# Two weight splits put off in a graph attention kernel, output sums moved behind a maximum, one split moved to GpSimd

## The chip, the cores and the metric

The kernel runs on one core of a Trainium2 chip. The metric is device time in microseconds (us) of one execution; lower is better. The profile is one execution recorded by the hardware profiler. Five engines work side by side, each through its own instructions in order: TensorE (PE; its weight loads are shown as PEld), VectorE (DVE), ScalarE (ACT), GpSimd (POOL) and SyncE (SP), which here only issues DMA transfers.

## The reference

A pre-norm graph attention layer on 384 nodes of 1024 features, with 16 heads of 64. Cut to what matters:

```python
h = maximum(layernorm(x), 0)
q = h @ wq.T + bq;  k = h @ wk.T + bk;  v = h @ wv.T + bv
q2 = (q @ wiq.T + biq).reshape(N, H, D).transpose(1, 0, 2)      # k2, v2 likewise
mask = full((N, N), -inf); mask[src, dst] = softplus(edge_type_weights)[edge_type - 1]
# diagonal cells without an edge get the fourth weight
attn = softmax(q2 @ k2.T / sqrt(D) + mask)
out = (attn @ v2) as (N, 1024)
return x + out @ wo.T + bo
```

## The kernel before

**Precision.** Every operand of the large products is cut into a high and a low part in a fast 32-bit matmul type, and each product is made of three matmuls (high by high, high by low, low by high; `mm3`, lines 367 to 369). A weight matrix comes in eight chunks of 128x1024 (512 KB). `load(w)` (line 65) starts the transfer of chunk `w` on SyncE's queue into one of three `raw` buffers; `split_hi(w)` (line 77) makes the high part on ScalarE, `split_lo(w)` (line 82) the low part on VectorE or, if so told, on GpSimd. Split chunks lie in four `whl` buffers. Because `raw` has three buffers, `load(w + 4)` fills the buffer of chunk `w + 1` and must wait for that chunk's low part.

**Chunks.** Numbers 0 to 31 are those of v, q, the second v and k. From `W0` = 32 the q2 and k2 chunks alternate: 32 + 2p is q2 of head pair p, 33 + 2p is k2. Numbers 48 to 55 are the output weights wo.

**Score phase.** A loop runs over steps i. Step i issues the scores S(i) (two matmuls, line 694) of head i // 3 and node block i % 3 in one of two PSUM banks `s`, then the masked maximum of step i-1 (`do_ttr`, line 700, VectorE), the exponential of i-2 (line 704, ScalarE), the normalization of i-3 (line 709, GpSimd), the transpose of i-5 (line 714), the split of the transposed probabilities of i-6 (lines 723 and 724) and, every third step, the product with v2 (line 731) and its evacuation (lines 741 and 742). Ahead of and behind S(i), a generator fills TensorE's time with other products, by a credit of about 8 per step: first `fill_qk` (the q2 and k2 chunks, 3 credits a block of `mm3`), then `fill_o` (the output product, 4 credits a block). Before step 0 `fill(PRE)` issues 28 blocks: chunks 32 to 34 and half of chunk 35.

**Work around a chunk.** At the start of chunk w's blocks `qk_head(w)` is put on a list, and run at once before step 0 or at the end of the step (`run_tasks`). It issues `load(w + 4)`, splits chunk w + 2 (low part on GpSimd for odd numbers, `PAR` = 1, on VectorE for even ones) and finishes the chunk before it: `qk_done` evacuates that chunk's sum to `nat` (lines 377 and 378), then rearranges it by four DMAs into `qs` (lines 557 to 560) or `ks` (line 567), which the scores read. All DMAs of the phase but four stand in SyncE's one queue in the order written.

**Output product.** It is made in two passes over the wo chunks: 0 to 3, then 4 to 7, for six output halves (three node blocks by two halves of 512 columns). The first pass ends for half a with `ysum(a)` (line 654, VectorE), which adds the PSUM sum onto a copy of x + bo in SBUF and so frees one of the three banks `g`. The last blocks of the first pass may start from step 43 (`XSTEP` + 3); x + bo is read back at step 40. `wo_prep(k)` splits wo chunk k at the steps in `WSTEPS`, k = 2 to 7 at 37, 40, 42, 44, 47, 51: the low part goes to GpSimd for k in `OPOOL` = (2, 3, 6), the high part to VectorE for k = 2. It then loads chunk k + 2.

## Time and profile before

| | us |
|---|---|
| median of three runs | 303.34 |
| lowest, highest of them | 301.37, 303.49 |
| the profiled execution | 302.19 |
| its span in the profile | 300.5 |

A line of the profile's timeline gives start and duration in us from the start of the span, engine, source line, operation, output<-inputs and shape, and in brackets the idle time before it and what ended it. A few matmul records can be missing, so a single gap of one matmul means nothing. The score phase lies between 160.85 (S0) and 270.9 (S47). What the engines did there, in two stretches around the changed places (columns: busy us and count for each engine, granted clock of TensorE, share of the DMA engines, GB/s):

```profile
165.00:170.00 5.00, 5.00 (x29) 4.70 (x29) 3.40 (x13) 3.33 (x8) 3.12 (x3) 1.00 1.06 223
260.00:265.00 5.00, 4.77 (x25) 3.62 (x23) 4.83 (x10) 3.25 (x9) 0.83 (x1) 1.00 0.69 260
```

The columns are PE, PEld, DVE, ACT, POOL. In the first the DMA engines are full, in the second VectorE nearly so and GpSimd nearly idle.

### The profile page before, as it was taken

The page shows a single profiled execution, that of the slowest core. Times are in us where ns is not written, and L with a number is a line of the kernel's source. Part 1 is how long each engine was busy: PE and PEld are TensorE (multiplying, and loading weights), DVE is VectorE, ACT ScalarE, POOL GpSimd, SP SyncE. Part 2 cuts the span into 40 slices and gives each one's busy share as a digit, 9 for nine tenths or more (in the row PEclk, how much of TensorE's full clock was granted, in tenths as well). Part 3 has the DMA queues.
Part 4 walks back from the last instruction along what each step waited for, and adds up shares of the span by engine and source line. Part 5 has one row for each costly group of instructions (what it writes and reads, how often), then busy time and mean ns, then how long its engine had stood idle before and what let it go on. Part 6 is the DMA issues. An engine that isn't in the chain of part 4 may idle for free.

```text
span 300.5 us, 4961 instructions
## 1 busy us (share of the span) xinstructions
PE 293.1 (98%) x1649; PEld 276.1 (92%) x1649; DVE 200.5 (67%) x492; ACT 154.9 (52%) x289; POOL 155.7 (52%) x164
## 2 busy tenths in 40 slices
PE   7899999999999999999999999999999999999995
PEld 5699999999988889999999999999999998888884
DVE  2959986655956463788865576767576757696523
ACT  3874644333422213554325667777777767676310
POOL 5865766271555785730033737373746467566210
PEclk9999999999999999999999999999999999999999
DMA  7899754642686668475369997646565636910005
GB/s 233 284 297 381 281 164 171 228 143 70 217 238 224 193 217 242 142 274 198 115 169 244 217 221 173 166 127 180 155 170 139 174 81 174 381 41 0 2 0 209
DMA packets 22377, 55.12 MB, mean 183 GB/s; under 512 B 4816, under 2 KB 8400, under 8 KB 22352
## 3 DMA queue, kind: packets, MB, share of 16 engines
q1 hardware_dynamic: 19968, 52.42, 57.7%
q0 software_dynamic: 2064, 1.80, 2.0%
q10 hardware_dynamic: 320, 0.59, 0.8%
q8 instruction: 13, 0.21, 0.3%
q14 instruction: 12, 0.10, 0.1%
HBM read 40.39 MB, written 4.97 MB: 151 GB/s over the span
## 4 chain that ended last, share of the span: by engine, by line
PE 95%; DMA 2%; DVE 1%; ACT 0%; issue 0%; SPq 0%
PE g L369 21%; PE g L367 21%; PE g L368 21%; PE s L694 6%; PE a L731 6%; PE t L714 5%; PE s L369 2%; PE s L368 2%; PE s L367 2%; DMA g<-in_x_dram 2%; PE t L369 2%; PE t L367 2%; PE t L368 2%; PE g L414 1%; PE a L369 1%; PE a L367 1%
## 5 line engine op out<-in xcount | busy, mean ns | idle before, releaser
L367 PE MATMUL g<-g,whl 128*128 128x384 f32 x312 | 106.4, 341 | 0.0
L369 PE MATMUL g<-g,whl 128*128 128x384 f32 x312 | 104.5, 335 | 0.0
L368 PE MATMUL g<-g,whl 128*128 128x384 f32 x312 | 104.2, 334 | 0.0
L228 POOL DMA_INDIRECT tab<-val,idx x51 | 57.6, 1129 | 40.3 <-issue 11.3
L77 ACT ACTIVATE whl<-raw 128x1024 fp32r<-128x1024 f32 x51 | 53.4, 1051 | 31.7 <-PE g L369 20.1
L709 POOL TENSOR_TENSOR e<-e,s 128x384 f32<-128x384 f32 x48 | 39.2, 830 | 41.2 <-DVE s L708 32.9
L368 PEld LDWEIGHTS g<-g,whl 128*128 128x128 f32 x312 | 58.7, 188 | 0.0
L367 PEld LDWEIGHTS g<-g,whl 128*128 128x128 f32 x312 | 58.6, 188 | 0.0
L369 PEld LDWEIGHTS g<-g,whl 128*128 128x128 f32 x312 | 58.5, 188 | 0.0
L82 DVE TENSOR_TENSOR whl<-raw,whl 128x1024 fp32r<-128x1024 f32 x41 | 50.2, 1224 | 9.6 <-ACT whl L77 7.9
L82 POOL TENSOR_TENSOR whl<-raw,whl 128x1024 fp32r<-128x1024 f32 x11 | 26.5, 2412 | 35.6 <-ACT whl L77 31.8
L383 ACT ACTIVATE g<-f,bc 128x384 fp32r<-128x384 f32 x24 | 14.8, 618 | 53.1 <-DVE f L382 46.8
L704 ACT ACTIVATE e<-e,s 128x384 f32<-128x384 f32 x48 | 29.4, 612 | 13.0 <-DVE s L700 13.0
L724 DVE TENSOR_TENSOR pt<-t,pt 128x384 fp32r<-128x384 f32 x48 | 26.4, 550 | 13.9 <-ACT pt L723 13.3
L723 ACT ACTIVATE pt<-t 128x384 fp32r<-128x384 f32 x48 | 23.2, 484 | 13.9 <-PE t L714 13.3
L700 DVE CUSTOM_DVE_ANT_0 e<-s,ma 128x384 f32<-128x384 f32 x48 | 26.3, 550 | 2.0 <-PE s L694 1.8
L694 PE MATMUL s<-ks,qs 128*128 128x384 f32 x96 | 25.3, 344 | 0.3 <-DVE s L700 0.2
L714 PE MATMUL t<-ident,e 128*128 128x128 f32 x144 | 23.5, 271 | 0.0
L382 DVE TENSOR_TENSOR f<-g,rrow 128x384 f32<-128x384 f32 x24 | 13.3, 555 | 13.5 <-PE g L369 7.6
L714 PEld LDWEIGHTS t<-ident,e 128*128 128x128 f32 x144 | 18.8, 140 | 3.1
L378 DVE SCALAR_TENSOR_TENSOR nat<-g,bc,nat 128x384 fp32r<-128x384 f32 x16 | 9.9, 618 | 16.4 <-ACT nat L377 14.4
L731 PE MATMUL a<-pt,vhl 128*128 128x384 f32 x96 | 20.8, 351 | 0.0
(147 smaller groups left out, 414.8 us busy)
## 6 DMA issues: line engine op xcount, KB each, us to landing
ks<-nat SPq DMA_DIRECT2D x30, 192.0 KB
raw<-in_wv_dram SPq DMA_DIRECT2D x8, 512.0 KB
raw<-in_wq_dram SPq DMA_DIRECT2D x8, 512.0 KB
raw<-in_wiv_dram SPq DMA_DIRECT2D x8, 512.0 KB
raw<-in_wk_dram SPq DMA_DIRECT2D x8, 512.0 KB
raw<-in_wiq_dram SPq DMA_DIRECT2D x8, 512.0 KB
raw<-in_wik_dram SPq DMA_DIRECT2D x8, 512.0 KB
raw<-in_wo_dram SPq DMA_DIRECT2D x8, 512.0 KB
```

The lines of the kernel that those rows point to most:

```text
L77: nc.scalar.activation(dst[0], raw[w], AF.Copy)
L82: (eng or nc.vector).tensor_tensor(lo, raw[w], hi.bitcast(F32), OP.subtract)
L228: nc.gpsimd.indirect_dma_start(out=tabs[c // RNG], out_offset=bass.IndirectOffsetOnAxis(ap=idx[:, c:c + 1], axis=0), in_=val[:, c:c + 1], ...
L367: nc.tensor.matmul(ps, lhi, rhi, start=first, stop=False)
L368: nc.tensor.matmul(ps, lhi, rlo, start=False, stop=False)
L369: nc.tensor.matmul(ps, llo, rhi, start=False, stop=last)
L694: nc.tensor.matmul(ps[:, :N], qs[:, o, t * 128:(t + 1) * 128], ks[:, o, s, :], start=(s == 0), stop=(s == 1))
L704: nc.scalar.activation(es[i], es[i], AF.Exp, bias=s[:, 0:1], scale=-1.0, accum_out=s[:, 1:2])
L709: nc.gpsimd.tensor_tensor(es[i], es[i], s[:, 2:3].to_broadcast([128, N]), OP.mult)
L714: nc.tensor.transpose(ps[:, k * 128:(k + 1) * 128], es[i][:, k * 128:(k + 1) * 128], ident)
L724: nc.vector.tensor_tensor(lo, pv, hi.bitcast(F32), OP.subtract)
L731: nc.tensor.matmul(ps[:, :N], vhl[:, k, p, 2 * o:2 * o + 2, :], pts[h][:, s, k, :], start=(k == 0 and s == 0), stop=(k == 2 and s == 1))
```

## The change

1. `qk_head` for chunks 35 and 36 no longer splits chunks 37 and 38 at once. It loads, finishes the chunk before, and notes the split for a later step: chunk 37 for the end of step 2 (noted before step 0), chunk 38 for the end of step 3 (noted in step 1).
2. `ysum(a)` of the first pass is noted in a list, and `flush_y` issues it behind the masked maximum of the step, or before a bank is taken for a new output half, whichever comes first.
3. wo chunk 4's low part goes to GpSimd: `OPOOL` = (2, 3, 4, 6).

TensorE's instructions and SyncE's DMAs stand in the same order in both programs.

```diff
+    defer = []
+
+    def qk_split(w):
+        split_hi(w)
+        split_lo(w, nc.gpsimd if w % 2 == PAR else None)
+
     def qk_head(w):
         first = w - W0 < 3
         if not first:
             load(w + 4)
+            if w - W0 < 5:
+                pendq.pop(0)()
+                defer.append((now[0] + 6 - w + W0, w + 2))
+                return
             split_hi(w + 2)
...
-    PAR, OPOOL, ODVE = 1, (2, 3, 6), (2,)
+    PAR, OPOOL, ODVE = 1, (2, 3, 4, 6), (2,)
...
+    ysums = []
+
+    def flush_y():
+        while ysums:
+            ysum(ysums.pop(0))
+
...
             if k == 0:
+                flush_y()
                 oacc[OT[a]] = bank("g")
             omm(*OT[a], k)
             if k == KH - 1:
-                ysum(a)
+                ysums.append(a)
             yield 4
...
             if k == KH:
+                flush_y()
                 oacc[OT[a]] = bank("gggss"[a])
...
             do_ttr(i - 1)
+        flush_y()
         if 0 <= i - 2 < S:
             do_exp(i - 2)
...
         run_tasks()
+        while defer and defer[0][0] <= i:
+            qk_split(defer.pop(0)[1])
```

## The prediction

> **What bounds the kernel now.** Read the page first, then TensorE's and its weight loads' timeline wherever a start is late, then the queues that release those starts.

> ```profile
> span 300.5 us, 4961 instructions
> PE 293.1 (98%) x1649; PEld 276.1 (92%) x1649; DVE 200.5 (67%) x492; ACT 154.9 (52%) x289; POOL 155.7 (52%) x164
> PE 95%; DMA 2%; DVE 1%; ACT 0%; issue 0%; SPq 0%
> ```

> The last line is the chain of waits: 95% of it is TensorE. The most a change of order can win is therefore the sum of TensorE's late starts. In the timeline a 384-column matmul follows the one before it after 0.173 us and a 512-column one after 0.23 us, at granted clock 1.00; a start later than that is a stall. The score steps have few, and these are those near the change:

> ```profile
> 166.19 0.30 PEld L694 LDWEIGHTS s<-ks,qs 128*128 128x128 f32 x2 [0.30 <-DVE s L700]
> 172.05 0.30 PEld L694 LDWEIGHTS s<-ks,qs 128*128 128x128 f32 x2 [0.36 <-issue]
> ...
> 262.30 0.40 PE L369 MATMUL g<-whl,g 128*128 128x512 f32 x1
> 262.92 0.62 PE L694 MATMUL s<-ks,qs 128*128 128x384 f32 x2 [0.23 <-DVE s L700]
> ...
> 264.86 0.40 PE L369 MATMUL g<-whl,g 128*128 128x512 f32 x1
> 265.24 0.62 PE L694 MATMUL s<-ks,qs 128*128 128x384 f32 x2
> ```

> The reader is to see four scores (L694) that start late: S3 (166.19), S6 (172.08 on TensorE), S44 (262.92), S45 (265.24). In start-to-start steps they cost: S3 0.319 - 0.173 and 0.284 - 0.173 for its second matmul, 0.26 together; S6 0.408 - 0.173 = 0.23; S44 0.625 - 0.23 and 0.282 - 0.173, 0.50; S45 0.374 - 0.23 and 0.11, 0.25. Scores have two PSUM banks, so S(i) waits for the masked maximum (L700) of i-2. VectorE shows what that one stands behind:

> ```profile
> 164.45 1.21 DVE L82 TENSOR_TENSOR whl<-raw,whl 128x1024 fp32r<-128x1024 f32 x1
> 165.58 0.55 DVE L700 CUSTOM_DVE_ANT_0 e<-s,ma 128x384 f32<-128x384 f32 x1
> ...
> 259.76 1.23 DVE L82 TENSOR_TENSOR g<-raw,g 128x1024 fp32r<-128x1024 f32 x1 [0.39 <-ACT g L77]
> 260.91 1.49 DVE L654 TENSOR_TENSOR g<-g,g 128x512 f32<-128x512 f32 x2
> 262.31 0.55 DVE L700 CUSTOM_DVE_ANT_0 e<-s,ma 128x384 f32<-128x384 f32 x1
> ```

> S3 waits behind the low part of chunk 38; S44 behind a wo low part and two output sums. S6 is another matter: its maximum was done at 170.7, and the profile says only "issue". It also waits for its K rows. By the trace's semaphore events the two DMAs with the first half of pair 1's K landed at 171.04 and 171.99, and S6 loaded its weights at 172.05: **a DMA wait**. SyncE's queue issued them so:

> ```profile
> 162.88 0.53 SPq L65 DMA_DIRECT2D raw<-in_wiq_dram  x1
> 164.56 2.64 SPq L567 DMA_DIRECT2D ks<-nat  x4
> 167.30 0.66 SPq L65 DMA_DIRECT2D raw<-in_wik_dram  x1
> ```

> [...]the load issued at 162.88 landed at 170.25, and K behind it at 171.04, 171.99, 173.15, 174.20. [...]The trace has a case: beside a GpSimd operation that took 2.00 us (L747, others 1.01), VectorE's L82 took 1.71 (usually 1.22). Maximum and output sum read one input from PSUM.

> **Part 1: splits of chunks 37 and 38 put off.** TensorE's and SyncE's orders stay as they were. On ScalarE hi(37) moves behind exponential 0 and hi(38) behind exponential 1; on VectorE lo(38) moves behind maxima 1 and 2; GpSimd's lo(37) keeps its place but waits for hi(37). Worked forward with durations of before:
> - ScalarE: pair 1's evacuations (L377) no longer stand behind the two splits, of which hi(38) waited for its load until 162.35. K of pair 1 (chunk 35) is evacuated when its matmuls end, about 162.4 instead of 163.3; exponential 0 about 162.9 to 163.6; hi(37) (1.05) to 164.6; exponential 1 to 165.3; hi(38) to 166.3.
> - VectorE: maximum 1 follows K's low evacuation, ending about 164.1 instead of 166.1. S3 starts on time: **-0.26**. lo(38) runs 166.3 to 167.5; behind it maximum 3 ends at 168.0, S5 (169.6 before) wants it at 169.3: covered. Chunk 38 is first multiplied near 174: covered.
> - GpSimd: lo(37) 164.6 to 167.0 (2.40) instead of 159.7 to 162.2. Normalizations 0 and 1 follow, done 168.7 (before 168.4); the first transpose needs one at 170.3: covered. lo(39) starts some 0.2 later. Chunk 37 is first multiplied with its low part at 168: 1 us of cover, the thinnest.
> - SyncE: load(40) takes chunk 37's buffer, so it waits for lo(37): issued about 167.0, not 162.9. Behind it in the queue are the four K DMAs of pair 1 (four times 0.66), load(41) (which also waits for lo(38), 167.5, less than its turn at 170.3), four Q DMAs of pair 2, load(42). K is then issued from 167.6 instead of 164.56. That is **the new cost**. Bounds for the K landing that S6 needs: the early one by a quiet stretch, where K issued at 190.94 had its second landing at 194.66, 3.72 later: 171.3. The late one is the whole shift of load(40), 171.99 + 4.1 = 176.1. Between: before, load(40) was issued into a backlog (DMA busy share about 1.0 from 160 to 180), and the Q DMAs ahead of it landed up to 168.04; a load in a quiet queue takes 3.25 (145.10 to 148.37). So load(40) lands near 170.3, about where it did, and K 0.8 and 1.0 after one another: second half at 172.1, range 171.8 to 172.8. I take 172.1.
> - S6 would be reached at 172.08 - 0.23 - 0.26 = 171.6; with K at 172.1 it starts at about 172.2. The 0.26 is given back in a longer stall: **S6 moves by +0.1** (at best -0.5, likely at most +0.8). Pair 2's Q and K have slack: K was issued at 176.15, when its evacuation was ready, and the queue has caught up by then (about 173.9 for load(42)).

> **Part 2: output sums behind the maximum.** Maximum 42 needs S42 (done 258.55) and VectorE is free at 259.4 with lo(wo 4) gone: it ends at 260.0, not 262.9. S44 starts on time: **-0.50**. First sum: its matmuls end near 260.65, so 260.65 to 261.3. Second: ends near 261.65, so to 262.35 as before. Then reciprocal, low part, head sum, third sum (0.69) to 264.15, and maximum 43 (0.55) at 264.1 to 264.7, 0.5 earlier than before. TensorE wants it for S45 0.50 earlier too: the 0.25 stall of S45 stays. The fourth output half takes the first one's bank, so its first matmul waits for the first sum (261.3); TensorE gets there near 262.9: covered. The later sums stand beside a maximum that was done 0.7 us before its score (269.8 for 270.53) or beside one that frees a bank for no score: nothing.

> **Part 3: lo(wo 4) on GpSimd.** 2.40 us at 259.7 to 262.1, in an idle stretch of 3.50 us (before 263.11, L709). Normalization 40 follows at 262.5. The chunk is used after 267. SyncE's last wo load waits for it, about 1.2 later (issued near 262.2); it is split at 278.76: covered. VectorE's work beside it has one PSUM input[...], and L82 on GpSimd at 255.64 slowed no maximum. A slowing would cost at most 0.5 (1.71 - 1.22)[...].

> **Sum**: +0.1 - 0.50 = -0.4 us (bounds -1.0 to +3.6). On the profiled execution 302.19 (span 300.5 and 1.69 around it) this is 301.8. That execution lies 1.15 below the median of three, 303.34; the median of all four is 302.77. I set the sum against that one: **302.4**.

> **Rivals.**
> - A, as worked out: -0.8 to +0.2 with the range of the landing, around 302.4. Chance 0.6.
> - B, K lands by 171.5: S6 keeps the whole gain, about -1.0, 301.8 on the same base. For it: the quiet 3.72. Against: load(40) goes first. 0.12.
> - C, slower: K stays behind load(40) late, at S6 alone. The change in time is (landing - 171.99) - 0.50, so it decides from a landing of 172.5. With 173.5 it is +1.0, 303.8; with the full shift +3.6, 306.4. For it: four microseconds of later issue. Against: the backlog that load(40) sat in anyway. 0.23, of which 0.03 is over 1%.
> - D, the stall of S44 passes to S45 whole, because the sums still come before maximum 43: +0.1, 302.9. Against: every term in that VectorE chain moves forward. 0.05.

> 1%, 3 us, is about what a measurement can tell here; runs of before differ by 2.1. All of A, B and D and most of C lie within it. A gain over 3 us has no place: the four stalls sum to 1.24. I leave 0.02 for the measurement. Faster 0.02, same 0.95, slower 0.03. The range adds the scatter of the runs to A and part of B and C: **301.0 to 304.2**.

> **What would show it.** S3 after 0.17, S44 after 0.23; S6's stall longer than 0.36 with load(40) issued near 167; S45 still late; GpSimd's low parts (L82) 13 instead of 12. Wrong if S6 starts later than 173 (C), or if chunk 37's multiplication waits for GpSimd.

## The result, and the profile after

| | before | after |
|---|---|---|
| median, us (runs) | 302.56 (22) | 304.81 (22) |
| lowest, highest | 301.37, 303.82 | 303.00, 307.99 |
| the profiled execution, span | 302.19, 300.5 | 303.63, 301.9 |

The change makes the kernel slower: ratio 1.0073, interval [1.0054, 1.0091], 2.25 us by the medians. The ratio is that of the runs without the two slowest, 307.70 and 307.99; the medians are of all runs. The page of the kernel after begins:

```profile
span 301.9 us, 4965 instructions
PE 292.5 (97%) x1649; PEld 276.2 (91%) x1649; DVE 200.4 (66%) x491; ACT 155.2 (51%) x289; POOL 162.0 (54%) x165
PE 92%; DMA 4%; ACT 1%; POOL 1%; DVE 1%; SPq 1%; issue 0%
```

TensorE does the same work in the same time and carries 92% of the chain of waits instead of 95%; DMA has 4% instead of 2%. In the timeline the scores have moved to line 712, the masked maximum to 718, the normalization to 727, the output sum to 664. Around S6 it shows:

```profile
165.36 2.41 POOL L82 TENSOR_TENSOR whl<-raw,whl 128x1024 fp32r<-128x1024 f32 x1 [8.97 <-ACT whl L77]
166.85 1.99 DVE L82 TENSOR_TENSOR whl<-raw,whl 128x1024 fp32r<-128x1024 f32 x1 [0.81 <-ACT whl L77]
167.79 0.33 SPq L65 DMA_DIRECT2D raw<-in_wiq_dram  x1
168.22 3.25 SPq L567 DMA_DIRECT2D ks<-nat  x4
...
172.13 0.34 PE L369 MATMUL g<-g,whl 128*128 128x384 f32 x1
173.94 0.59 PE L712 MATMUL s<-ks,qs 128*128 128x384 f32 x2 [1.47 <-DMA ks<-nat]
```

This execution runs 0.72 us later than that of before from S0 on (161.57 against 160.85), which is no work of the change: the experiment below that only exchanges two transfers of the kernel before at a later place starts as late. In the four profiles at full clock with no edit ahead of S0 (before, and three of the experiments) S0 lies anywhere from 160.85 to 161.70. So 0.72 is subtracted when the two are compared. GpSimd makes chunk 37's low part at 165.36; SyncE can issue load(40) only at 167.79, and the four K DMAs of pair 1 behind it from 168.22. S6 follows the matmul at 172.13 after 1.81 us, where before took 0.408. By the trace's semaphore events load(40) landed at 172.30, the two first K halves at 173.07 and 173.85.

The DMA view for 166 to 175 us has 40 slices of 0.225 us; a digit is the busy share of the 16 DMA engines in tenths. Before:

```profile
DMA  8998999999999999999999999999997997999999
```

After:

```profile
DMA  5321000000008959898799999899999999999999
```

The reader is to see the zeros: from about 166.9 to 168.7 the DMA engines had nothing to do, because SyncE's queue stood still at the wait for chunk 37's low part.

At the other place, the maximum comes first and both sums follow. The score at 262.36 is S43, S44 is the one at 264.43, 0.234 after the matmul before it, and S45 the one at 266.66:

```profile
261.19 0.55 DVE L718 CUSTOM_DVE_ANT_0 e<-s,ma 128x384 f32<-128x384 f32 x1
262.36 0.51 PE L712 MATMUL s<-ks,qs 128*128 128x384 f32 x2
262.56 0.69 DVE L664 TENSOR_TENSOR g<-g,g 128x512 f32<-128x512 f32 x1 [0.81 <-PE g L369]
263.60 0.69 DVE L664 TENSOR_TENSOR g<-g,g 128x512 f32<-128x512 f32 x1 [0.35 <-PE g L369]
264.43 0.52 PE L712 MATMUL s<-ks,qs 128*128 128x384 f32 x2
...
266.66 0.30 PEld L712 LDWEIGHTS s<-ks,qs 128*128 128x128 f32 x2 [0.42 <-DVE s L718]
```

The sum for the profiled executions: S6 +1.40 (1.81 - 0.408), S3 -0.26, S44 -0.50, the later start +0.72, together +1.36 of the 1.44 between 303.63 and 302.19. But the profiled execution is one of the fastest of its kernel. The median lies 1.2 higher, and eight of the 22 runs have a mean granted clock of TensorE of 0.994 or 0.989 instead of 1.00. The medians by clock are 304.55 (13 runs at 1.00), 306.13 (6 at 0.994) and 307.85 (2 at 0.989); one run at 0.998 took 304.02. Of before's 129 runs beside all the experiments, 19 are at 0.994 or below. So two questions are open: is it load(40) ahead of K, and what does the clock do?

### The profile page after: what moved, and what is told of

Same layout as the page of the kernel before. It is cut to its first block, busy times and chain, and to the rows that moved or that the text cites. A ratio compares the mean times of both kernels' runs of the same rounds, so it can differ in the third digit from the quotient of the medians.

```text
span 301.9 us, 4965 instructions
## 1 busy us (share of the span) xinstructions
PE 292.5 (97%) x1649; PEld 276.2 (91%) x1649; DVE 200.4 (66%) x491; ACT 155.2 (51%) x289; POOL 162.0 (54%) x165
## 4 chain that ended last, share of the span: by engine, by line
PE 92%; DMA 4%; ACT 1%; POOL 1%; DVE 1%; SPq 1%; issue 0%
PE g L367 21%; PE g L369 21%; PE g L368 20%; PE a L749 6%; PE s L712 5%; PE t L732 5%; DMA g<-in_x_dram 2%; PE s L368 2%; PE s L369 2%; PE s L367 2%; DMA ks<-nat 2%; PE t L369 2%; PE t L368 2%; PE t L367 2%; PE g L414 1%; POOL whl L82 1%
## 5 line engine op out<-in xcount | busy, mean ns | idle before, releaser
L369 PE MATMUL g<-g,whl 128*128 128x384 f32 x312 | 104.5, 335 | 0.0
L228 POOL DMA_INDIRECT tab<-val,idx x51 | 60.2, 1181 | 36.0 <-DMA tab<-val,idx 12.1
L77 ACT ACTIVATE whl<-raw 128x1024 fp32r<-128x1024 f32 x51 | 53.5, 1051 | 28.8 <-PE g L369 15.0
L82 DVE TENSOR_TENSOR whl<-raw,whl 128x1024 fp32r<-128x1024 f32 x41 | 51.1, 1246 | 12.1 <-ACT whl L77 12.1
L369 PEld LDWEIGHTS g<-g,whl 128*128 128x128 f32 x312 | 58.5, 188 | 0.0
L727 POOL TENSOR_TENSOR e<-e,s 128x384 f32<-128x384 f32 x48 | 40.3, 851 | 33.6 <-DVE s L726 25.2
L82 POOL TENSOR_TENSOR whl<-raw,whl 128x1024 fp32r<-128x1024 f32 x11 | 26.5, 2406 | 41.2 <-ACT whl L77 37.5
L712 PEld LDWEIGHTS s<-ks,qs 128*128 128x128 f32 x96 | 17.2, 188 | 3.5 <-issue 1.8
```

The costliest lines, as they stand in the source:

```text
L77: nc.scalar.activation(dst[0], raw[w], AF.Copy)
L82: (eng or nc.vector).tensor_tensor(lo, raw[w], hi.bitcast(F32), OP.subtract)
L228: nc.gpsimd.indirect_dma_start(out=tabs[c // RNG], out_offset=bass.IndirectOffsetOnAxis(ap=idx[:, c:c + 1], axis=0), in_=val[:, c:c + 1], ...
L369: nc.tensor.matmul(ps, llo, rhi, start=False, stop=last)
L712: nc.tensor.matmul(ps[:, :N], qs[:, o, t * 128:(t + 1) * 128], ks[:, o, s, :], start=(s == 0), stop=(s == 1))
L727: nc.gpsimd.tensor_tensor(es[i], es[i], s[:, 2:3].to_broadcast([128, N]), OP.mult)
```

## The experiments

**The change again, with a profile**, and the first part alone.

> The changed kernel once more, for a second profile and its scatter. Theory K (the load of chunk 40 waits for chunk 37's late low part and holds up pair 1's K behind it in SyncE's queue): ratio about 1.007, and the one long TensorE stall of the score phase is at S6 (1.6 us over the usual step in the first profile, at least 1.5 here); a slower execution has a longer one. Rival D (GpSimd and VectorE in each other's way once both low parts run together, 1.99 us for chunk 38's instead of 1.21): the time goes in several places, with TensorE waiting for L82 before chunks 37 or 38.

> Part 1 alone: splits of chunks 37 and 38 put off, sums and wo low part as before. Theory K: all of the loss and none of the 0.5 us that part 2 wins, so about 2.7 us above the kernel before (ratio 1.009). If parts 2 and 3 were what costs: at or below 1.000.

The second is the kernel after with parts 2 and 3 taken back:

```diff
-                ysums.append(a)
+                ysum(a)
...
-    PAR, OPOOL, ODVE = 1, (2, 3, 4, 6), (2,)
+    PAR, OPOOL, ODVE = 1, (2, 3, 6), (2,)
```

Measured: the change again 305.98, ratio 1.0126 [1.0080, 1.0172]; part 1 alone 306.59, ratio 1.0116 [1.0081, 1.0151]. Part 1 carries the whole loss, as far as six runs of each tell. In the profiles load(40) is issued at 167.63 and 167.54, as in the first profile, but lands at 173.15 and 174.17; S6 starts 2.80 and 3.93 after the matmul before it. The longer the wait, the slower the profiled execution: 303.63, 306.01 and 307.50. And something follows that the first profile lacks. TensorE with part 1 alone, up to S6, and in the repeat:

```profile
171.87 0.34 PE L369 MATMUL g<-g,whl 128*128 128x384 f32 x1
175.80 0.58 PE L712 MATMUL s<-ks,qs 128*128 128x384 f32 x2 [3.59 <-DMA ks<-nat]
```

```profile
171.96 0.34 PE L369 MATMUL g<-g,whl 128*128 128x384 f32 x1
174.76 0.59 PE L712 MATMUL s<-ks,qs 128*128 128x384 f32 x2 [2.46 <-DMA ks<-nat]
175.19 0.34 PE L367 MATMUL g<-g,whl 128*128 128x384 f32 x1
...
178.01 0.52 PE L367 MATMUL g<-g,whl 128*128 128x384 f32 x1
178.33 0.52 PE L368 MATMUL g<-g,whl 128*128 128x384 f32 x1
...
179.35 0.34 PE L369 MATMUL g<-g,whl 128*128 128x384 f32 x1
```

In the repeat a 384-column matmul took 0.34 before the stall and just after it, then 0.52, with 0.32 from start to start instead of 0.173, and 0.34 again from 179.18. The view by stretches (PE, PEld, DVE, ACT, POOL, clock, DMA share, GB/s) has the granted clock in the third figure from the right:

```profile
176.00:178.00 2.00, 2.00 (x8) 2.00 (x7) 0.58 (x2) 1.35 (x3) 0.83 (x1) 0.50 1.09 238
```

In the trace half clock lasts 3.41 us here and after part 1's stall too. By estimate that costs half of it, about 1.7 us, and explains a mean clock of 0.994 (1 - 1.7/304); from S6 to S44 the repeat took 92.06, the first profile 90.49, 1.57 less. The idle time ahead of S6 was 2.46 in the repeat and 3.59 with part 1 alone; behind the 1.47 of the first profile the clock stayed at 1.00. With the half clock the profiled repeat adds up: S6 +2.39, S3 and S44 -0.76, half clock +1.57, start +0.55, together +3.75 of the 3.82 between 306.01 and 302.19.

How long TensorE stood idle ahead of half clock can be read from the twelve profiles. In each of them the granted clock changes only at whole multiples of 3.413 us from the trace's first record of full clock: in before at 6.45 and 299.99, 86 of them later; in the first profile of after at 5.51 and 302.47, 87 later; in the repeat at 4.96, then 175.62, 50 later, and 179.04. Cut into these stretches, which begin at another time in each profile, the profiles show what each stretch held of TensorE's work and which clock came next:

| profile, stretch | matmul busy, us of 3.41 | clock of the next stretch |
|---|---|---|
| the repeat, 172.21 to 175.63 (S6's wait) | 0.96 | 0.50 |
| part 1 alone, 173.41 to 176.82 (S6's wait) | 1.02 | 0.50 |
| parts 2 and 3 alone (below), 8.56 to 11.98 | 1.46 | 0.50 |
| only chunk 38 put off (below), 8.39 to 11.81 | 1.59 | 0.50 |
| the repeat, 8.37 to 11.79 | 1.76 | 1.00 |
| the first profile, 172.77 to 176.18 (S6's wait) | 2.24 | 1.00 |

All ten stretches with 1.59 us or less (the other six lie at the end of the execution) were followed by half clock, and none of the 1021 with 1.76 or more was. So in these profiles half clock went with the work in one such stretch, and with where the stretch began, not with the length of a gap alone: near 9 us, gaps of 1.83 and 1.97 us lie in the two stretches that were followed by half clock, and one of 2.13 us, in the profile of part 3 alone, is cut in two by the boundary at 9.98 and was not. These two lie at the start of the kernel, before anything that was edited; a mean clock of 0.994 does not say where the clock was lost.

**K first.** The kernel after with load(40) issued behind the K DMAs of pair 1; nothing else is moved.

```diff
-            load(w + 4)
+            if w - W0 != 4:
+                load(w + 4)
             if w - W0 < 5:
                 pendq.pop(0)()
+                if w - W0 == 4:
+                    load(w + 4)
```

> The changed kernel with the load of chunk 40 put behind pair 1's four K DMAs; the wait of that load for chunk 37's low part stays. Theory K: K is issued near 163.9 as soon as it is evacuated, its second landing comes by 171, S6 starts without a stall, and with S3 and S44 also in time the kernel is 1.0 us below the kernel before (ratio 0.9967). Rival D: the low parts still overlap, so the time stays at 1.007. Rival Q (the DMA engines are simply full and K lands at 173 to 174 in any order): also about 1.007.

Measured: 301.75, ratio 0.9965 [0.9950, 0.9979]. SyncE's queue and S6's weight load:

```profile
164.42 2.41 SPq L567 DMA_DIRECT2D ks<-nat  x4
167.79 0.33 SPq L65 DMA_DIRECT2D raw<-in_wiq_dram  x1
...
172.14 0.37 PEld L715 LDWEIGHTS s<-ks,qs 128*128 128x128 f32 x2
```

load(40) is issued at the same 167.79 and lands at 172.34, as late as in the change, and nobody misses it. K lands at 167.37 and 168.15, and S6, S3 and S44 start on time. One run of 22 is at 0.994. So it is the place of K behind the late load(40), not load(40)'s own lateness, nor the low part on GpSimd, nor that both low parts run at once.

**The same on the kernel before, and on part 1 alone.** The edit is the same; in the kernel before, load(40) follows the call that finishes the chunk before.

> The kernel before with the load of chunk 40 behind pair 1's K. Prediction's reading of S6 (it waits for K's second landing, not for a maximum): its 0.23 us stall goes, K's second landing near 169, ratio 0.999. Rival (S6 waits for the maximum): no difference in S6's start, ratio 1.000; these two are told apart by the profile, hardly by the time.

> Part 1 alone with the load of chunk 40 behind pair 1's K; sums and wo low part as before. Theory K: splits put off are worth the 0.49 us of S3 and S6 once K is free, ratio 0.998, with S44 late as before (0.5 us). If it is 1.003 or more, putting the splits off costs something besides K.

Measured: before with K first 302.57, ratio 0.9994 [0.9978, 1.0011]; part 1 with K first 302.38, ratio 0.9994 [0.9981, 1.0006]. In the first S6's stall is gone (K landed at 167.80 and 168.96), those of S3 (0.276 and 0.278 from start to start) and S44 (0.625) are there. In the second S3's is gone too, S44's still 0.625. That S6 waited for K in the profile of before rests on the landing, 171.99, and the weight load, 172.05; this pair of runs alone would not show it. Three profiles below with load(40) ahead of K as in before (parts 2 and 3, and each alone) have no stall at S6 either: K had landed at 171.83, 170.97 and 172.05, and S6 started at 173.52, 172.22 and 172.78. S3's stall varies as well where chunk 38 is split at once, from nothing to 0.34, and is absent in all seven profiles where that split is put off. So the 0.49 us that part 1 was to win is what one execution of before had lost. In the time neither shows: 0.23 and 0.49 us lie within these intervals, which reach 0.4 to 0.5 us each way.

**Only chunk 38 put off.** Parts 2 and 3 stay; chunk 37 is split at once as before, so load(40) doesn't wait.

```diff
-            if w - W0 < 5:
+            if w - W0 == 4:
```

> Chunk 37 is split at once as in the kernel before, chunk 38 put off as in the changed one, sums and wo low part as changed. Theory K: the load of chunk 40 goes out near 163, K lands as before (172.0), S6 stalls some 0.5 us over the step, no long stall: ratio 0.998, at most 1.000. If putting off chunk 38 were the costly one: 1.005 or more.

Measured: 301.70, ratio 0.9971 [0.9959, 0.9984]. load(40) is issued at 164.49 in a profile whose S0 starts at 162.52 (the half clock at its start), K lands at 172.19 and 173.27, S6 follows after 0.270. Of the two deferrals it is that of chunk 37 that costs.

**Parts 2 and 3 without part 1**, then each alone.

```diff
-            if w - W0 < 5:
+            if False:
```

> Parts 2 and 3 alone: sums behind the maximum and the wo low part on GpSimd, splits of 37 and 38 as before. Theory K and the prediction: S44 in time, S45 late by 0.25 still, 0.5 us below the kernel before (ratio 0.998). Rival: GpSimd's longer work shows later and the ratio is 1.002 or more.

Measured: 302.06, ratio 0.9975 [0.9956, 0.9993]. S44 starts on time, S45 after 0.384: the gain that was forecast for S44. For the parts alone the kernel before got only the list of sums, or only the new `OPOOL`.

> The kernel before with only the output sums put behind the masked maximum; wo chunk 4's low part stays on VectorE. Theory (the sums are what holds S44): maximum 42 stands behind the low part alone and ends near 261.6 on the profile's time of before, under 1 us ahead of S44's turn (262.5): S44 starts on time, S45 keeps its stall, -0.5 us, ratio 0.9983. Rival (the low part on VectorE is what holds S44, the sums only fill its shadow): S44 still starts 0.3 or more late, ratio 1.000.

> The kernel before with only the low part of wo chunk 4 on GpSimd; the sums stay ahead of the maximum. Theory (the sums hold S44): they wait for their own matmuls, which end near 260.65 and 261.65, so maximum 42 still ends near 262.9, S44 stays 0.3 to 0.4 late: ratio 1.000. Rival (the low part holds S44): the stall is gone, ratio 0.9983.

Measured: the sums alone 302.38, ratio 0.9986 [0.9972, 1.0000]; the low part alone 302.77, ratio 0.9995 [0.9981, 1.0008]. With the low part alone, the second sum waits for its matmuls, and the maximum and S44 for that sum, as the theory had it (lines as in the kernel before):

```profile
262.34 0.69 DVE L654 TENSOR_TENSOR g<-g,g 128x512 f32<-128x512 f32 x1 [0.35 <-PE g L369]
262.95 0.55 DVE L700 CUSTOM_DVE_ANT_0 e<-s,ma 128x384 f32<-128x384 f32 x1
...
263.56 0.62 PE L694 MATMUL s<-ks,qs 128*128 128x384 f32 x2 [0.23 <-DVE s L700]
```

With the sums alone the theory missed S45. VectorE and TensorE in that profile:

```profile
260.96 0.55 DVE L718 CUSTOM_DVE_ANT_0 e<-s,ma 128x384 f32<-128x384 f32 x1
261.44 1.28 DVE L664 TENSOR_TENSOR g<-g,g 128x512 f32<-128x512 f32 x2
...
264.48 0.55 DVE L718 CUSTOM_DVE_ANT_0 e<-s,ma 128x384 f32<-128x384 f32 x1
...
265.09 0.61 PE L712 MATMUL s<-ks,qs 128*128 128x384 f32 x2 [0.26 <-DVE s L718]
```

S44 is on time, but VectorE, with the low part's 1.23 us still to do, works without a pause from there to the next maximum at 264.48. S45 starts after 0.656 instead of 0.374: 0.28 of the 0.50 is passed on, which was rival D's mechanism. Only both parts together keep the whole 0.50.

**TensorE kept busy in the wait.** The kernel after with 16 transposes that nobody reads put ahead of S6, so that TensorE stands idle for a shorter time though S6 starts no earlier.

```diff
+        if i == 6:
+            ps = bank("a")
+            for _ in range(16):
+                nc.tensor.transpose(ps[:, :128], ident, ident)
```

> The changed kernel with 16 transposes of the identity into the idle bank a just ahead of S6, about 1.5 us of TensorE work whose result nobody reads. K's landing is not touched. Theory C (a stall of 2.6 us and more lets TensorE's clock be halved for 3.4 us, as two of the profiles show, and that is up to 1.7 us of the loss and its scatter): median falls by 0.5 to 1.2 us against the changed kernel, no execution above 306, clock 1.00 behind S6. Rival (the halved clock costs nothing that counts, or comes anyway): median the same or higher by up to 1.5 us where the stall was shorter.

Measured: 305.17 (304.27 to 305.64), ratio 1.0080 [1.0057, 1.0103]. The profile:

```profile
172.36 1.91 PE L792 MATMUL a<-ident 128*128 128x128 f32 x16
175.29 0.59 PE L712 MATMUL s<-ks,qs 128*128 128x384 f32 x2 [1.02 <-DMA ks<-nat]
```

Load(40) landed late in it (174.16), and S6 started 3.1 after the matmul ahead of the transposes (172.18), longer than in the repeat. Yet the clock stays at 1.00 in every stretch from 168 to 182. One run of six is at 0.994, against eight of 22, five of six and five of six in the three kernels with the open wait. The median is 0.8 under the repeat's, but not under the first 304.81. By the table above the stretch from 173.20 to 176.61 held 2.39 us of work, of which 1.07 were transposes; without them it would have held 1.32 (an estimate), less than every stretch that kept the clock. So in this profile the clock stayed at 1.00 with part of the idle time filled, though S6 came no earlier. That filling it shortens the run is not shown at six runs, when one and the same kernel gave 304.81 and 305.98.

## Why the prediction was wrong

**The step that failed** is "load(40) lands near 170.3, about where it did", from "a load in a quiet queue takes 3.25". In the four profiles in which load(40) waited for the late low part with K behind it, it landed 4.51, 5.52, 6.64 and 6.32 us after its issue; in the first that is at 172.30, or 171.58 with the 0.72 subtracted, 1.3 later than forecast. The first of the 16 DMA engines was done with it 2.7 to 3.0 after the issue each time (170.53 to 170.73), the last at 172.30, 173.15, 174.17 and 174.16, and these last times are the landings. The queue was quiet, as forecast; the zeros show it. But a quiet queue was not all that the price needed.

The 3.25 was no lucky draw: the 24 loads that the twelve profiles issue between 140 and 147.5 us all landed in 3.10 to 3.36. What sets load(40) apart is one packet. In all four profiles a packet of 8192 bytes of an instruction queue starts 1.0 to 1.8 us after load(40)'s issue and takes 0.90 to 1.97 us (169.62 and 0.90 in the first). Among the loads of 512 KB from 20 us on that found the DMA engines idle (no packet from 0.3 us before the issue to 0.9 after), 77 had no packet of an instruction queue within 3 us of the issue and landed in 3.04 to 3.90; 11 had one, these four and seven near 82 us, and landed in 4.51 to 6.64. In three of the four, one engine alone came 1.5 to 2.7 us behind the one before it; in the first profile the engines came in one after another. No run moved such a packet, so that it is what holds the last engine back is not shown.

All around that step held:
- chunk 37's low part at 164.6 to 167.0: 165.36 to 167.77, less 0.72;
- load(40) issued about 167.0: 167.79, less 0.72;
- K 0.8 after the load, and its second half 1.0 after that: 0.77 and 0.78;
- S6 reached at 171.6: the matmul before it started at 172.13, plus 0.173, less 0.72.

So S6's "+0.1" (its stall, less what S3 gives back) was +1.14 in the first profile (1.40 - 0.26) and +2.13 in the repeat (2.39 - 0.26); with S44's -0.50, which came as forecast, the sum "-0.4" was +0.64 and +1.63 before the clock. The runs of the kernel after at clock 1.00 have a median of 304.55, before's 110 runs at 0.997 or more 302.55. The 2.0 between them lies within what the four landings give by the formula of rival C: 0.64, 1.63, 1.93 and 2.76.

**Rival C** was the right mechanism. Its formula, (landing - 171.99) - 0.50, gives 0.64 with the landing measured (173.85 less 0.72), what the stalls sum to. I gave it 0.23 against the backlog argument, with its far end at 0.03.

**The clock was a term put at nothing.** In every case of the prediction a stall was priced at its own length. Steps to S6 of 2.80 and 3.93 us were followed by 3.41 us at half clock, 1.6 to 1.7 more. By their mean clock eight of the 22 runs lost as much, two of them twice that, though a part of this may come from elsewhere, as in 19 of before's 129 runs and in the two profiles with half clock near 12 us.

**What held.** S3's stall went (-0.26) and S44's (-0.50), S45's stayed (0.385 after 0.374), K of later pairs came in time, chunk 37's low part kept nobody waiting on TensorE. VectorE's two output sums beside GpSimd's low part of wo chunk 4 (261.71 to 264.12) took 0.69 each, as the one at 265.44 did with no GpSimd work beside it; why they were not slowed is not shown. Putting the 0.50 down to part 2 was half right: it needs part 3, which alone is worth nothing. Two sizes were off with no consequence that the trace shows: the low part of chunk 38 on VectorE took 1.99, not 1.21, 0.9 of it beside GpSimd's of chunk 37, and the prediction had a case of the kind, 1.71 beside GpSimd's L747; and the first two normalizations took 2.65 together, not 1.7, so lo(39) starts about 1.1 later than in before, not 0.2.

## What to carry to other kernels

Where work that frees a buffer is put off, look at every transfer that stands behind the refill in the same queue: here SyncE issued K at 168.22, only behind load(40) at 167.79, and a late load that harmed nobody by itself (172.34 with K first) made K late (173.85, against 168.15 with K first). Issuing what is needed first ahead of the load that waits takes the loss away (0.9965 here). The gain that is left comes from parts 2 and 3: alone they gave 0.9975, and that putting the splits off adds to it is not shown. Price a landing by the last of the DMA engines (172.30 in the first profile, with the first at 170.53), and by loads that have the same company on them. Price a TensorE stall with what the clock may lose after it: by the table, an otherwise busy stretch of 3.41 us can be followed by half clock once about 1.8 us of it are idle (an estimate, 3.41 - 1.59); with up to 1.65 idle (3.41 - 1.76) none was.
